# Layer 0's second product on four column groups of 32: a four-layer NHWC kernel on one Trainium2 core

## The chip, the cores and the metric

The kernel runs on one core of a Trainium2 chip. The metric is the device time of one execution in microseconds. Beside it there is one profiled execution, from which all rows and views in this document come. Engines are called as in the profile: PE is the matrix engine, PEld its weight loads, DVE, ACT and POOL the three elementwise engines, SP the engine that issues the DMAs.

## What is computed

The input is `x` of 32 images of 56 x 56 tokens with 96 channels, f32, and it goes through four layers. Only layer 0 is touched, and of it only its last product:

```python
rw = sigmoid(mean(x, (1, 2)) @ Wr + br)                 # 4 weights an image
h = relu(bn(x @ mix(rw, Wpw) + ..))                     # 96 -> 384 channels
h = relu(bn(depthwise 3x3 of h, mixed by rw))           # 384 channels
Wk2 = einsum('be,emf->bmf', rw, Wpwl)                   # 384 x 96, one an image
out = bn(h @ Wk2 + ..) + x                              # 384 -> 96, and the shortcut
```

Layer 1 is a depthwise 5x5 filter with a residual, layer 2 a depthwise 3x3 and a pointwise product, layer 3 a shifted-window attention block with a perceptron.

## The kernel before

Every image passes through four stages, each a generator: `stage_router` (the means, the mixed weights), `stage_conditional` (the rest of layer 0), `stage_depthwise` (layers 1 and 2) and `stage_swin` (layer 3). Four images are under way at a time, one in each stage.

**The order of the work** is not that of the code. Every call is recorded as a `Work` with a target, its due time in units of images; `interleave` and `PLAN` (a start and a length for each stage) give these targets. `Recorder.order` then plays all engines through with a table of costs (`COST`, `tensor_time`, `BESIDE`, and the lags `CROSSING` and `TO_TENSOR` between engines) and lets each engine, whenever it is free, begin the ready work with the earliest target whose buffers are available. What comes out is the order in which each engine's instructions are emitted, and on the chip an engine keeps to it. Three rules of this planner matter here:

- Where PE has nothing that could start, the planner emits products of the identity with itself (`banks<-ident` in the profile), whose results nobody reads. I call them spare products.
- An elementwise instruction of DVE over 500 ns that has all its operands in SBUF is never followed by another such: another DVE instruction comes between, or else a memset of one element (`breath`).
- Calls inside `chip.together()` are one piece of work and stay together. PE pays `CHANGE` in the plan when the size of its tiles changes.

**Layer 0's second product.** `stage_conditional` cuts an image into 2 strips of 28 rows. For each strip it makes three blocks of 128 channels, each with nine taps: ACT does the first, DVE the other eight (`h<-h,mix,h`, 128 x 1568). The three blocks of a strip (`h2`, four buffers) are then multiplied with `wmix2`, 3 x (128 x 96), in four pieces of 7 rows, that is 392 columns: `project(n)` accumulates three products of 128 x 96 into one PSUM bank, and `add(n)` lets DVE add the bias and the shortcut out of that bank into `xT`. The generator `projections` yields after each product and after each add, so their targets are spread over the taps of the following block (of the next strip, or after the last one). In f32 one product is two PE records in the trace. All stages draw on one ring of six PSUM banks (`mm` and `cv` are the same ring); the band filters of layers 1 and 2 take four of them at once, the attention scores three. When all pieces of an image are in `xT`, SP copies it in 48 DMAs to the layout of layer 1.

All recorded instructions have line 578 (`Recorder.give`), so in this document they are told apart by their tiles: `banks<-h,wmix` is the second product, `banks<-xT,wmix` the first, `xT<-banks,bias,xT` the add.

Of the kernel before, what the change touches and what calls it, by code (L numbers as in the profile page):

```python
# [19 lines left out]
C = 96  # L20
# [3 lines left out]
P = 128  # L24
NB = 3
NROW = 8
RT = 7 * W
# [17 lines left out]
NSTRIP = H // STRIP  # L45
# [113 lines left out]
LANDING = 2200  # L159
IMAGE_LANDING = 10000  # L160

PLAN = {"router": (-0.309, 1.019), "conditional": (0.642, 1.103), "depthwise": (1.462, 1.483), "swin": (3.316, 0.933)}
CROSSING = 136

TO_TENSOR = {"vector": 981, "gpsimd": 1497, "scalar": 453, "sync": 1437}
SPARE_AFTER = 318
RUN = 1
CHANGE = 170
SAME = 0.0
BESIDE = {(32, 32): 16, (32, 64): 6, (64, 32): 6, (32, P): 3, (P, 32): 3, (P, P): 1}  # L170


def up(n):
# [3 lines left out]
def tiling(call):  # L177
    return tuple(up(n) for n in call[1][1].shape[:1] + (math.prod(call[1][1].shape[1:]),))


def tensor_time(calls):

    tiles = BESIDE[tiling(calls[0])]
    total = 30 if tiles > 1 else 0
# [107 lines left out]
class Recorder:  # L292
# [79 lines left out]
    def order(self):  # L372
# [50 lines left out]
        def done(w, now):  # L423
# [5 lines left out]
            for v in w.after:  # L429
                v.waits -= 1  # L430
                lag = 0 if v.engine == w.engine else TO_TENSOR[w.engine] if v.engine == "tensor" else CROSSING
                v.ready = max(v.ready, now + lag)
# [42 lines left out]
        while left:  # L475
            for e in self.ENGINES:
# [5 lines left out]
                while queues[e] and not unchanged:  # L482
                    item = heapq.heappop(queues[e])
                    w = self.work[item[1]]
                    if not available(w):
                        held.append(item)
                        continue
                    if e == "tensor" and SAME:
                        if first is None:
                            first = item  # L490
                        if item[0] > first[0] + SAME:
                            held.append(item)
# [89 lines left out]
def kernel(  # L582
# [10 lines left out]
    def ring(name, shape, n):  # L593
        return Ring([const.tile(shape, F32, name=f"{name}{k}") for k in range(n)])
# [21 lines left out]
    x1s = ring("x1", [P, NQ, NBLK, W + 4], 2)  # L616
    x2s = ring("x2", [P, NQ, NBLK, W + 2], 2)
    filtereds = ring("filtered", [C + 1, H, W], 1)
    h1s = ring("h1", [P, STRIP + 2, W + 2], 2)
    if general:  # L620
        ss = ring("scores", [PK, NP, PK], 4)
# [55 lines left out]
    for k in range(NB):  # L677
        pt = mm.tiles[k]
# [16 lines left out]
    pt = mm.tiles[3]  # L695
# [31 lines left out]
    pt = mm.tiles[5]  # L727
# [27 lines left out]
    pt = mm.tiles[4]  # L755
# [87 lines left out]
    chip = Recorder(nc)  # L843
# [66 lines left out]
    def stage_conditional(b):  # L910

        xT, wmix, wmix2, mix, bias1, biasd, bias3 = mixed.pop(b)
        h1s_of = {}
        pieces = STRIP // 7

        def expand(strip, k):

            h1 = h1s_of[strip, k] = chip.new(h1s).part(*range(pieces))
            edge = 0 if strip == 0 else STRIP + 1
            chip.gpsimd.memset(h1[:, edge], 0.0)  # L920
            first = max(0, STRIP * strip - 1)
            last = min(H, STRIP * strip + STRIP + 1)
            at = first - (STRIP * strip - 1)
            for piece in range(pieces):
                n = -(-(last - first) // (pieces - piece))
                pt = chip.new(mm)
                chip.tensor.matmul(
                    pt[:, : n * W],
                    wmix[:, k * P : (k + 1) * P],
                    xT[:, first * W : (first + n) * W].part(*range(first // 7, (first + n - 1) // 7 + 1)),  # L930
                    start=True,
                    stop=True,
                )
                chip.scalar.activation(
                    h1[:, at : at + n, 1 : W + 1].part(piece),
                    pt[:, : n * W].rearrange("p (r w) -> p r w", w=W),
                    AF.Relu,
                    bias=bias1[:, k : k + 1],
                    scale=s1[:, k : k + 1],
                )  # L940
                first += n
                at += n
                yield

        def project(n, h2):

            pt = chip.new(mm)
            with chip.together():
                for q in range(NB):
                    chip.tensor.matmul(  # L950
                        pt[:C, :RT],
                        wmix2[:, q * C : (q + 1) * C],
                        h2[q][:, n % pieces * RT : (n % pieces + 1) * RT].part(n % pieces // 2),
                        start=(q == 0),
                        stop=(q == NB - 1),
                    )
            return pt[:C, :RT]

        def add(n, y):
            rows = xT[:, 7 * n * W : 7 * (n + 1) * W].part(n)  # L960
            chip.vector.scalar_tensor_tensor(rows, y, bias3, rows, ALU.add, ALU.add)

        def projections(strip, h2):
            for n in range(pieces * strip, pieces * (strip + 1)):
                y = project(n, h2)
                yield
                add(n, y)
                yield

        blocks = [(strip, k) for strip in range(NSTRIP) for k in range(NB)]
        for _ in expand(*blocks[0]):
            pass
        yield 2
        def relu(acc, k):
            for half in range(2):
                part = acc[:, half * 2 * RT : (half + 1) * 2 * RT].part(half)
                chip.scalar.activation(part, part, AF.Relu, bias=biasd[:, k : k + 1], scale=s2[:, k : k + 1])

        behind = iter(())
        filtered_before = None
        h2 = {}
        for at, (strip, k) in enumerate(blocks):
            ahead = expand(*blocks[at + 1]) if at + 1 < len(blocks) else iter(())
            h1 = h1s_of[strip, k]
            h2[k] = chip.new(h2s).part(0, 1)
            acc = h2[k].rearrange("p (r w) -> p r w", w=W)
            for t in range(9):
                dy, dx = divmod(t, 3)  # L990
                tap = mix[:, k, t : t + 1]
                view = h1[:, dy : dy + STRIP, dx : dx + W]
                if t == 0:
                    chip.scalar.activation(acc, view, AF.Copy, scale=tap)
                else:
                    chip.vector.scalar_tensor_tensor(acc, view, tap, acc, ALU.mult, ALU.add)
                yield 2
                if t % 2 == 0:
                    next(ahead, None)
                    yield 1  # L1000
                if t == 1 and filtered_before:
                    relu(*filtered_before)
                if t > 1:
                    next(behind, None)
                    yield 1
            filtered_before = h2[k], k
            if k == NB - 1:
                for _ in behind:
                    yield 1
                behind = projections(strip, dict(h2))  # L1010
        yield 4
        relu(*filtered_before)
        yield 1
        for _ in behind:
            yield 1
        added[b] = xT
# [579 lines left out]
    def when(stage, b):  # L1596

        start, length = PLAN[stage]
        return b + start, length
# [5 lines left out]
    for step in range(B + 3):  # L1605
        stages = []
        b = step - 3
        if 0 <= b < B:
            stages.append((stage_swin(b, residuals.pop(b)), 148.5, when("swin", b)))
        b = step - 2  # L1610
        if 0 <= b < B:
            residuals[b] = []
            stages.append((stage_depthwise(b, residuals[b]), 49, when("depthwise", b)))
        b = step - 1
        if 0 <= b < B:
            stages.append((stage_conditional(b), 195, when("conditional", b)))
        if step < B:
            stages.append((stage_router(step), 12, when("router", step)))
        interleave(stages)
# [3 lines left out]
def build(nc, shapes, batch):  # L1623

    a = {k: nc.dram_tensor(f"in_{k}", s, F32, kind="ExternalInput").ap() for k, s in shapes.items()}
    layouts = {
        k: nc.dram_tensor(f"in_{k}", s, F32, kind="ExternalInput").ap()
        for k, s in (
            ("mask", (2, PK, NP, PK)), ("keep_last", (P, NP, WT)), ("keep_column", (P, WT)),
            ("k5", (P, NSLOT, 5, 2 * BIN)), ("k3", (P, NSLOT, 3, 2 * BIN)), ("centre", (P, 2 * BIN)),  # L1630
        )
    }

    out = nc.dram_tensor("out", (batch, NROW // 2, 2 * RT, C), F32, kind="ExternalOutput").ap()
    with tile.TileContext(nc) as tc, tc.tile_pool(name="flags", bufs=1) as flags:
        in_range = flags.tile([1, 1], mybir.dt.int32, name="in_range")
        tile_scores_in_range(tc, a, in_range)
        kernel(tc, a, layouts, out, False)

        with tc.If(nc.values_load(in_range[:1, :1]) < 1):  # L1640
            kernel(tc, a, layouts, out, True)
# [23 lines left out]
```

## Time and profile before

| what | value |
|---|---|
| median of 3 runs | 4646.62 us (4646.44 to 4652.35) |
| the profiled execution, its own time | 4639.04 us |
| its span, first to last instruction | 4637.2 us |
| mean granted PE clock | 0.992 of full |
| PE busy | 4489.9 us, 97% |
| DVE busy | 4061.4 us, 88% |
| ACT busy | 3393.6 us, 73% |
| POOL busy | 2967.1 us, 64% |

A group row reads: line, engine, operation, output<-inputs, rows*columns of the PE tile, output shape<-input shape, count | busy us, mean ns of one | idle time of the engine just before them, and what ended most of it. A PE record's duration is a latency through the array; records overlap, so the pace of PE is read from the distance between the starts. A timeline row reads: start us, length us, engine, and a run of equal records, merged. A window row gives, for a stretch of the span, each engine's busy us and, in brackets, its count of instructions.

### The profile page before, as it was taken

The numbers are of one execution on the slowest core, as the hardware profiler recorded it, in microseconds if no ns is written. First come the engines' busy times: TensorE is split into PE (matmuls) and PEld (weight loads), VectorE is DVE, ScalarE is ACT, GpSimd is POOL, SyncE is SP. The second block draws the span as 40 slices with busy tenths as digits, with TensorE's granted clock in tenths as the row PEclk, the third lists the DMA queues.
The fourth block names the chain that finished last, engine by engine and source line by source line (L and its number), as shares of the span: only waits on it lengthen the run. The fifth ranks groups of instructions, "written<-read, shape, count | busy, mean of one in ns | idle before, by whom it ended". The sixth has DMA issues, their size and how long they took to land. (4 is left out here: it accounts for less than half of the span.)

```text
span 4637.2 us, 166483 instructions
## 1 busy us (share of the span) xinstructions
PE 4489.9 (97%) x71978; PEld 3168.6 (68%) x71978; DVE 4061.4 (88%) x5444; ACT 3393.6 (73%) x6625; POOL 2967.1 (64%) x1855
## 2 busy tenths in 40 slices
PE   5799999999999999999999999999999999999999
PEld 3566767676767676666676766666766676766677
DVE  6999999998999998999998999988999999999733
ACT  2467777777777777777787777777777787777666
POOL 3035767666767766767766767766767666767633
PEclk8999999999999999999999999999999999999999
DMA  2112111122111122211121211121211122211110
GB/s 54 34 39 45 41 43 32 39 48 45 44 41 30 38 47 45 45 40 30 38 47 45 46 40 30 38 45 45 46 41 30 38 45 45 46 41 31 28 36 22
DMA packets 556411, 185.36 MB, mean 40 GB/s; under 512 B 551679, under 2 KB 552340, under 8 KB 552596
## 3 DMA queue, kind: packets, MB, share of 16 engines
q1 hardware_dynamic: 555668, 174.61, 16.9%
q8 instruction: 569, 9.32, 0.9%
q14 instruction: 174, 1.43, 0.1%
HBM read 42.37 MB, written 38.54 MB: 17 GB/s over the span
## 5 line engine op out<-in xcount | busy, mean ns | idle before, releaser
L578 DVE SCALAR_TENSOR_TENSOR h<-h,mix,h 128x1568 f32<-128x1568 f32 x1536 | 2892.2, 1890 | 18.7 <-ACT h L578 13.0
L578 POOL TENSOR_TENSOR var<-var,mhalf 112x4 f32<-112x4 f32 (+1 forms) x512 | 1068.8, 2093 | 195.4 <-DVE var L578 182.8
L578 POOL TENSOR_TENSOR lnd<-res,var 112x384 f32<-112x384 f32 (+1 forms) x512 | 779.1, 1528 | 524.7 <-PE banks L578 503.0
L578 ACT ACTIVATE hid<-banks,c 128x448 f32<-128x448 f32 (+1 forms) x768 | 446.4, 589 | 346.5 <-PE banks L578 340.4
L578 PE MATMUL banks<-xT,wmix 96*128 96x392 f32 (+1 forms) x1536 | 644.2, 519 | 5.7 <-DVE wmix L578 4.5
L578 PE MATMUL banks<-hT,w 96*128 96x448 f32 (+1 forms) x1536 | 641.0, 507 | 3.7
L578 PE MATMUL banks<-x,band 32*32 32x280 f32 x24576 | 611.7, 408 | 14.8 <-issue 7.7
L578 PEld LDWEIGHTS banks<-w,hid 128*112 128x112 f32 x5376 | 563.9, 178 | 75.9 <-issue 46.2
L578 POOL TENSOR_TENSOR tb<-res,L_conv_b 112x384 f32<-112x384 f32 (+1 forms) x256 | 506.3, 1994 | 160.0 <-DMA out<-tb 139.1
L578 PE MATMUL banks<-w,hid 128*112 128x96 f32 x5376 | 576.2, 262 | 5.1 <-ACT hid L578 4.6
L578 PE MATMUL banks<-h,wmix 128*96 128x392 f32 x1536 | 548.4, 497 | 11.6 <-ACT h L578 11.6
L578 ACT ACTIVATE h<-banks,bias,s 128x392 f32<-128x392 f32 (+1 forms) x768 | 518.3, 690 | 39.0 <-PE banks L578 29.6
L578 PEld LDWEIGHTS banks<-x,band 32*32 32x32 f32 x24576 | 385.0, 103 | 226.7 <-issue 50.7
L578 POOL TENSOR_TENSOR exps<-exps,keep_column 49x147 f32<-49x147 f32 x224 | 396.2, 1769 | 204.1 <-ACT exps L578 194.0
L578 ACT ACTIVATE h<-h,biasd,s 128x784 f32<-128x784 f32 x384 | 389.3, 1038 | 114.0 <-DVE breath L578 83.6
L578 PEld LDWEIGHTS banks<-h,wmix 128*96 128x96 f32 x1536 | 246.5, 164 | 248.6 <-issue 207.2
L578 PEld LDWEIGHTS banks<-xT,wmix 96*128 96x128 f32 x1536 | 266.0, 192 | 134.0 <-issue 57.6
L578 DVE TENSOR_REDUCE var<-lnsq 112x4 f32<-112x388 f32 (+1 forms) x512 | 253.7, 496 | 113.3 <-ACT lnsq L578 59.8
L578 ACT ACTIVATE h<-h,mix 128x1568 f32<-128x1568 f32 x192 | 308.6, 1607 | 60.4 <-PE banks L578 46.4
L578 DVE SCALAR_TENSOR_TENSOR tb<-banks,res,tb 112x96 f32<-112x96 f32 x896 | 246.6, 308 | 109.2 <-PE banks L578 103.9
L578 PEld LDWEIGHTS banks<-hT,w 96*128 96x128 f32 x1536 | 252.5, 191 | 128.9 <-issue 69.1
L578 PEld LDWEIGHTS banks<-ident,lnd 112*96 112x96 f32 x1792 | 197.5, 126 | 157.0 <-issue 127.3
(135 smaller groups left out, 6653.0 us busy)
## 6 DMA issues: line engine op xcount, KB each, us to landing
x<-xT SPq DMA_DIRECT2D x1536, 35.0 KB
xT<-in_x SPq DMA_DIRECT2D x32, 1176.0 KB
filtered<-x SPq DMA_DIRECT2D x960, 35.0 KB
out<-tb SPq DMA_DIRECT2D x128, 168.0 KB
out<-tb SPq DMA_DIRECT2D x128, 126.0 KB
filtered<-x SPq DMA_DIRECT2D x576, 7.0 KB
band<-in_k SPq DMA_DIRECT2D x1, 960.0 KB
wpw<-in_L_conv_Wpw SPq DMA_DIRECT2D x1, 576.0 KB
```

Source lines behind the costliest of these rows:

```text
L578: getattr(getattr(self.nc, w.engine), method)(*args, **kw)
```

## The change

`project` becomes `round_of`. Three rounds a strip replace the four pieces. In each round PE's columns are four groups of 32. Groups 0 to 2 (PSUM partitions 0 to 95) compute piece r, 32 output channels each; group 3 (partitions 96 to 127) computes 32 channels of the fourth piece, those of group r. After three rounds the fourth piece is complete, spread over three banks. ACT copies its three parts from partitions 96 to 127 into a new SBUF tile `last` (96 x 392, one buffer), and DVE adds it from there. The three rounds of a strip are recorded one after the other, with one target; the adds of the first three pieces and the copies follow at later targets, the add of the fourth piece, but for the last strip, three steps later still. Beside that, seven constants of the planner are changed: the starts and lengths of three stages, the lags, the number of 128 x 32 tiles that go beside each other (3 to 4), and `SAME`, which at 0.0003 lets PE prefer, among work whose targets lie that close, work of the tile size it has.

```diff
-PLAN = {"router": (-0.309, 1.019), "conditional": (0.642, 1.103), "depthwise": (1.462, 1.483), "swin": (3.316, 0.933)}
-CROSSING = 136
+PLAN = {"router": (-0.215, 1.029), "conditional": (0.618, 1.103), "depthwise": (1.457, 1.478), "swin": (3.316, 0.951)}
+CROSSING = 177
-TO_TENSOR = {"vector": 981, "gpsimd": 1497, "scalar": 453, "sync": 1437}
+TO_TENSOR = {"vector": 1024, "gpsimd": 1444, "scalar": 453, "sync": 590}
-SAME = 0.0
-BESIDE = {(32, 32): 16, (32, 64): 6, (64, 32): 6, (32, P): 3, (P, 32): 3, (P, P): 1}
+SAME = 0.0003
+BESIDE = {(32, 32): 16, (32, 64): 6, (64, 32): 6, (32, P): 3, (P, 32): 4, (P, P): 1}
...
+    lasts = ring("last", [C, RT], 1)
...
-        def project(n, h2):
+        def round_of(r, h2):
             pt = chip.new(mm)
             with chip.together():
-                for q in range(NB):
-                    chip.tensor.matmul(
-                        pt[:C, :RT],
-                        wmix2[:, q * C : (q + 1) * C],
-                        h2[q][:, n % pieces * RT : (n % pieces + 1) * RT].part(n % pieces // 2),
-                        start=(q == 0),
-                        stop=(q == NB - 1),
-                    )
-            return pt[:C, :RT]
+                for k in range(NB):
+                    for at in range(pieces):
+                        n, g = (r, at) if at < pieces - 1 else (pieces - 1, r)
+                        chip.tensor.matmul(
+                            pt[32 * at : 32 * at + 32, :RT],
+                            wmix2[:, k * C + 32 * g : k * C + 32 * g + 32],
+                            h2[k][:, n * RT : (n + 1) * RT].part(n // 2),
+                            start=(k == 0),
+                            stop=(k == NB - 1),
+                        )
+            return pt
...
         def projections(strip, h2):
-            for n in range(pieces * strip, pieces * (strip + 1)):
-                y = project(n, h2)
+            last = chip.new(lasts)
+            pts = []
+            for r in range(pieces - 1):
+                pts.append(round_of(r, h2))
+            yield
+            for r, pt in enumerate(pts):
+                chip.scalar.copy(last[32 * r : 32 * r + 32].part(r), pt[32 * (pieces - 1) :, :RT])
+                add(pieces * strip + r, pt[:C, :RT])
                 yield
-                add(n, y)
+            for _ in range(3 if strip < NSTRIP - 1 else 0):
                 yield
+            add(pieces * strip + pieces - 1, last.part(*range(pieces - 1)))
+            yield
```

## The prediction

> **What bounds the kernel now.** I read the page first, for the shares of the engines over the span; then the busy time by windows, for the stretches with different limits; then PE's waits and its group rows in the steady stretch; last PE's timeline, for the pace of single products. The chain of waits ends after one link and says nothing here.
>
> ```profile
> PE 4489.9 (97%) x71978; PEld 3168.6 (68%) x71978; DVE 4061.4 (88%) x5444; ACT 3393.6 (73%) x6625; POOL 2967.1 (64%) x1855
> ...
> PE   5799999999999999999999999999999999999999
> ...
> DVE  6999999998999998999998999988999999999733
> ```
>
> PE is full from the fourth slice to the end. DVE is nearly full for most of that, but idle at the end.
>
> ```profile
> 0.00:120.00 120.00, 64.63 (x298) 47.02 (x298) 81.29 (x163) 38.19 (x50) 34.86 (x37) 0.89 0.21 53
> 120.00:377.00 257.00, 220.95 (x3075) 150.52 (x3074) 244.53 (x270) 140.85 (x251) 60.29 (x49) 0.93 0.16 34
> 377.00:4360.00 3983.00, 3939.52 (x64040) 2764.15 (x64038) 3624.94 (x4775) 3038.99 (x5937) 2758.05 (x1638) 1.00 0.18 41
> 4360.00:4637.00 277.00, 264.82 (x4571) 206.94 (x4570) 110.68 (x239) 175.56 (x391) 113.87 (x132) 0.98 0.12 28
> ```
>
> Up to 377 us the pipeline fills, and DVE is the fuller engine (244.5 of 257 us from 120 on). From 377 to 4360 us PE is busy 98.9%, DVE 91.0%, ACT 76%. The router's reduce `pooled`, one an image, starts first at 560.3 and last at 4170.0 us with 26 images between: a period of 138.8 us. Is the busy PE a needed PE? For 560 to 4170 us:
>
> ```profile
> PE pair L578 <- DVE oT L578: 15.3, 26, 0.6
> PE banks L578 <- issue: 7.2, 17, 0.9
> ...
> L578 PE MATMUL banks<-ident 128*128 128x128 f32 x520 | 67.2, 276 | 0.0
> ```
>
> PE's longest wait in 26 periods sums to 15.3 us, and the spare products take 67.2 us, 2.6 us a period. With the 1.1% of idle time (1.5 us) some 4 of 138.8 us are not needed. So in the steady stretch PE's work sets the period, and work taken off PE shortens it, as long as DVE follows. Where DVE could not is seen inside one period:
>
> ```profile
> 1985.00:2005.00 20.00, 19.95 (x375) 13.01 (x374) 19.31 (x21) 18.40 (x43) 18.38 (x11) 1.00 0.05 10
> 2005.00:2026.00 21.00, 20.30 (x418) 15.60 (x417) 20.18 (x24) 18.26 (x39) 15.67 (x7) 1.00 0.07 16
> 2026.00:2040.00 14.00, 14.00 (x161) 8.02 (x160) 13.44 (x19) 6.26 (x14) 13.07 (x8) 1.00 0.06 14
> ...
> 2108.00:2124.00 16.00, 16.00 (x83) 10.51 (x82) 13.62 (x33) 9.93 (x16) 6.58 (x6) 1.00 0.18 44
> ```
>
> The first three rows are attention: DVE is busy 52.9 of 55 us, and all spare products of this period are there. The second strip's pieces run in the third row (2026 to 2039 us), the first strip's in the last (2108 to 2123 us), where DVE is at 85%.
>
> **PE's time for the product.** The timeline gives its pace now, and that of products on small tiles:
>
> ```profile
> 2026.44 2.14 PE L578 MATMUL banks<-h,wmix 128*96 128x392 f32 x6
> 2028.51 0.55 PE L578 MATMUL pair<-exps,ones 49*32 49x196 f32 x12
> 2028.86 0.66 PE L578 MATMUL pair<-exps,v 49*32 49x49 f32 x48
> ...
> 2054.09 3.88 PE L578 MATMUL banks<-x,band 32*32 32x280 f32 x160
> 2057.91 0.55 PE L578 MATMUL pair<-exps,ones 49*32 49x196 f32 x12
> ...
> 2119.26 4.12 PE L578 MATMUL banks<-h,wmix 128*96 128x392 f32 x12
> 2123.21 0.55 PE L578 MATMUL banks<-ident,lnd 112*96 112x112 f32 x4
> ```
>
> Two pieces, 12 records, take 2123.21 - 2119.26 = 3.95 us, 0.329 us a record, which is 1191 columns a us. A strip (24 records) takes 7.90 us. The piece at 2026.44, followed by another tile size, takes 2.07 us, 0.10 more: the price of one change of size.
>
> After, a strip has 3 rounds x 3 blocks x 4 groups x 2 = 72 records of the same 392 columns. One at a time they would take 23.7 us, four abreast 5.93 us. The trace has no 128 x 32 tile, so these are the bounds. Two rows lie near. The 12 records at 2028.51 (three column groups, two row groups; 196 columns, 0.165 us each) take 0.35 us to the next start: 12 x 0.165 / 0.35 = 5.7 abreast of 6. The 160 band records (all 16 tiles; 280 columns, 0.235 us each) take 3.82 us: 9.8 abreast of 16. But these start 24 ns apart on average, and 16 abreast would need 15 ns; the new ones need only 82 ns, so the pace of issue that may hold the band back does not bear on them. I take four abreast, by the first row. Two changes of size (0.2 us) and the lag of the groups behind one another at the start of a round (the starts of `exps,ones` lie 7 ns apart: under 0.1 us in three rounds) make 6.2 us. **A strip saves 7.9 - 6.2 = 1.7 us of PE, an image 3.4 us.** The weight loads triple in number; those of 32 columns take 103 to 106 ns, beneath passes of 329 ns, as today's of 164 ns are.
>
> A rule speaks against this. The Trainium skill, "TensorE: Matmul & The Clock Gate", section "Measured speedup vs the span model", gives 2.38 times for three column tiles and 3.07 times for four row tiles, not 3 and 4. By 3.07 the rounds would take, as an estimate from that page, 23.7 / 3.07 = 7.7 us and with the changes of size save nothing. The row above, 5.7 of 6 in a run of small-tile products, speaks for the higher figure, but it has three column groups and not four.
>
> **How much of that the end sees.** Of the 64 strips six have their products before 377 us (they start at 98, 150, 199, 247, 297 and 366 us), where DVE sets the pace: nothing. Of the 58 others, 29 first strips lie where DVE has room: 29 x 1.7 = 49 us. The 29 second strips lie in attention, right after the spare products. There a saving turns partly into more spare products unless DVE keeps up, and DVE has 55.0 - 52.9 = 2.1 us to give. I count half: 25 us. Together 74 us.
>
> Does DVE allow it over the whole period? It is busy 126.5 us of these 139 us (all eight windows from 1985 to 2124 us), and would be at 126.5 / 135.6 = 93%. Yes, but with little left.
>
> **The other parts.** *ACT* gets 6 copies an image. The nearest row, 96 x 392 out of a bank, is 0.49 us: 2.9 us an image, into 24% of idle time. If that cover went, 64 x 1.5 = 94 us would be in play; nothing points to it. *DVE* has eight adds as before (0.617 us); two now read SBUF alone, like `hid<-hid,hid` at 0.636 us: +0.04 us an image. They also count as long SBUF operations and each may draw a `breath` of 59 ns: 0.1 us at most. *Banks*: today four banks are taken one after another, each until its add; after, three at nearly one time, each until its copy and its add. Bounds: nothing, or PE waiting a strip for one tap of DVE (1.89 us) to let a bank go. I take nothing, since ACT and the adds empty them in the same order. *`h2`* is released earlier (one yield instead of seven after the strip's end), which can only help. *SP*: the 48 DMAs of an image wait for the last add; its chain becomes longer by a copy of 0.5 us, while the products before it end sooner. Nothing. *The constants* move everything a little. Upwards they can give no more than the 4 us a period that PE doesn't need (29 periods: 116 us). Downwards: the lag from a DMA to PE falls by 847 ns in the plan, and PE may be put to wait for a landing at three band filters and one pointwise product an image, 4 x 0.85 x 29 = 98 us. PE has 43 changes of tile size a period; what `SAME` spares of them is 0.1 us each. I take nothing for the sum, and keep both ends.
>
> **Sum.** The profiled execution took 4639.0 us by its own time (span 4637.2): 4639 - 74 = 4565 us. The median of the runs is 7.6 us above that execution, so 4646.6 - 74 = **4573 us**, 1.6% less.
>
> **The rivals.**
> 1. *Everything is gained*: the planner puts taps of DVE elsewhere, so the second strips gain in full: 58 x 1.7 = 99 us, and some of the 4 us with it: 4520 to 4555 us. For it: DVE idles 12% from 2040 to 2124 us. Against: the attention windows.
> 2. *DVE becomes the bound*, or the rounds are torn apart (six changes of size a strip, 0.4 us lost): 10 to 49 us are left, 4598 to 4636 us. For it: DVE at 96% in attention.
> 3. *Four column groups don't run abreast* (slower). At the band's share, 9.8 of 16, it would be 2.45 abreast: 23.7 / 2.45 + 0.2 = 9.9 us a strip, 2.0 us more than now, 58 x 2.0 = +116 us: 4763 us. It decides below 23.7 / (7.9 - 0.2) = 3.1 abreast. For it: that band row is the only one with four column groups. Against: its pace of issue.
> 4. *PE waits in its fixed order*, for banks or for landings (slower): 58 x 1.89 - 74 = +36 us, 4682 us. For it: full PE gets no time back. Against: PE's waits now sum to under 40 us in 26 periods.
>
> **How the numbers follow.** About the forecast (4555 to 4598) 0.42; rival 1, 0.19; rival 2, 0.14; within 0.2% (9 us, which is about what a measurement of this kernel can tell from no change) 0.07; rival 3, 0.08; rival 4, 0.10. Faster 0.75, same 0.07, slower 0.18. The range from 4515 (rival 1 and a little of the slack) to 4655 leaves out rivals 3 and 4.
>
> **What would show it.** A group `banks<-h,wmix` with 128\*32 and 4608 records; a strip's 72 records in about 6.1 us from first start to next work (right), or over 7.7 us (rival 3). The period from `pooled` at 135 to 137 us. Spare products up from 2.6 us a period by about 1 to 2 us, in attention: the half that I don't count. DVE at 93% in the steady stretch. Rival 4 would stand as idle time of PE, ended by ACT, DVE or a DMA, where now it is 1.5 us a period. The prediction is wrong if the strip takes 6.2 us and the period doesn't fall.

## The result, and the profile after

The changed kernel takes 4767.39 us (median of four runs, 4752.77 to 4775.44), the kernel before beside it 4646.53 us (four runs, 4641.05 to 4652.35). The ratio is 1.0256, 95% interval 1.0232 to 1.0281: **slower by 121 us**, where I forecast 74 us faster. The profiled execution is the longest of the four, 4775.44 us; its span is 4773.6 us, 136 us longer than before's.

First the page's line of busy times and the row of the granted clock:

```profile
PE 4512.6 (95%) x75444; PEld 3159.3 (66%) x75444; DVE 4107.2 (86%) x5130; ACT 3458.0 (72%) x6817; POOL 2530.4 (53%) x1855
...
PEclk8889999999999999899999999999999999999999
```

No engine took over: PE, DVE and ACT all have a smaller share than before, and PE is busy 23 us longer. Then the steady stretch, the same window as in the prediction:

```profile
377.00:4360.00 3983.00, 3838.39 (x65068) 2666.93 (x65067) 3561.43 (x4317) 2998.73 (x5918) 2253.75 (x1580) 0.98 0.18 40
```

From 377 to 4360 us PE is now busy 3838 instead of 3940 us, so it idles 145 instead of 43 us; DVE falls from 91 to 89%.

**The product itself** did what was forecast. PE's timeline has a whole strip:

```profile
2091.05 6.13 PE L578 MATMUL banks<-h,wmix 128*32 128x392 f32 x72
2097.11 0.55 PE L578 MATMUL pair<-exps,ones 49*32 49x196 f32 x12
```

72 records take 6.06 us from their first start to the next work; 72 x 0.329 us one at a time would be 23.7 us, so 3.9 run abreast. The Trainium skill, "TensorE: Matmul & The Clock Gate", section "Measured speedup vs the span model", states 2.38 times for three column tiles and 3.07 for four row tiles. It has no figure for four column tiles; this row lies above both figures, and it decides here.

**The period** did not follow. `pooled` starts at 602.6 us (before 560.3) and, 26 images later, at 4312.2 us (before 4170.0): 142.7 us an image, not 138.8. Before, the 26 distances lie between 137.7 and 140.1 us; after, between 123.2 and 162.8 us. The regular schedule has become an irregular one. The longer period makes 100 us of the 136, the later start 42, the end gives 6 back.

PE's waits between 602 and 4312 us, against the two rows shown in the prediction (us in total, times, longest):

```profile
PE pair L578 <- DVE oT L578: 40.5, 52, 2.5
PE banks L578 <- ACT slots L578: 39.0, 67, 1.4
PE banks L578 <- issue: 19.6, 23, 2.6
PE banks L578 <- ACT hid L578: 15.2, 26, 1.1
```

The wait for `oT` was 15.3 us and never over 0.6 us; `slots` did not appear. The spare products in this stretch rise from 520 records and 67.2 us to 868 and 143.4 us. But for the `issue` row, in which the profile shows nothing that PE waited for, all of this is time in which the order has nothing useful for PE. The clock follows from such places. PE's timeline:

```profile
1948.62 2.25 PE L578 MATMUL banks<-ident 128*128 128x128 f32 x14
1953.15 0.90 PE L578 MATMUL pair<-exps,ones 49*32 49x196 f32 x12 [2.28 <-DVE oT L578]
```

and two windows around it, the last but two columns being the granted clock:

```profile
1944.00:1953.00 9.00, 6.82 (x154) 5.18 (x146) 9.00 (x12) 4.13 (x8) 0.68 (x1) 1.00 0.18 39
1953.00:1960.00 7.00, 6.85 (x88) 6.50 (x89) 6.50 (x7) 2.81 (x6) 4.35 (x1) 0.50 0.26 59
```

At the end of a wait of 2.28 us the clock falls to 0.50, and stays so for 23.9 us. Between 377 and 4350 us the records of the clock show 133 us at one half, before none.

### The profile page after: what moved, and what is told of

It is laid out like the page before. It is cut to its first block, busy times and chain, and to the rows that moved or that the text cites. A ratio compares the mean times of both kernels' runs of the same rounds, so it can differ in the third digit from the quotient of the medians.

```text
span 4773.6 us, 173133 instructions
## 1 busy us (share of the span) xinstructions
PE 4512.6 (95%) x75444; PEld 3159.3 (66%) x75444; DVE 4107.2 (86%) x5130; ACT 3458.0 (72%) x6817; POOL 2530.4 (53%) x1855
## 5 line engine op out<-in xcount | busy, mean ns | idle before, releaser
L578 POOL TENSOR_TENSOR var<-var,mhalf 112x4 f32<-112x4 f32 (+1 forms) x512 | 946.4, 1855 | 502.1 <-DVE var L578 488.5
L578 POOL TENSOR_TENSOR lnd<-res,var 112x384 f32<-112x384 f32 (+1 forms) x512 | 705.6, 1383 | 206.0 <-PE banks L578 194.0
L578 POOL TENSOR_TENSOR exps<-exps,keep_column 49x147 f32<-49x147 f32 x224 | 280.6, 1253 | 622.2 <-ACT exps L578 590.8
L578 ACT ACTIVATE h<-banks,bias,s 128x392 f32<-128x392 f32 (+1 forms) x768 | 507.1, 693 | 102.2 <-PE banks L578 63.5
L578 POOL TENSOR_TENSOR tb<-res,L_conv_b 112x384 f32<-112x384 f32 (+1 forms) x256 | 409.0, 1605 | 305.1 <-DMA out<-tb 221.4
L578 PEld LDWEIGHTS banks<-xT,wmix 96*128 96x128 f32 x1536 | 280.0, 197 | 197.9 <-issue 79.8
L578 PE MATMUL banks<-h,wmix 128*32 128x392 f32 x4608 | 402.3, 496 | 8.3 <-ACT h L578 8.3
L578 PEld LDWEIGHTS banks<-h,wmix 128*32 128x32 f32 x4608 | 141.9, 110 | 243.3 <-issue 210.5
L578 PE MATMUL banks<-ident 128*128 128x128 f32 x1640 | 259.1, 295 | 36.5 <-ACT h L578 23.5
```

The costliest lines, as they stand in the source:

```text
L578: getattr(getattr(self.nc, w.engine), method)(*args, **kw)
```

## The experiments

Theory A: the new constants give a worse order, the product is innocent. Theory B: the new product (rounds kept together, banks held longer, copies by ACT) costs it. Theory C: the order is so sensitive that neither can be blamed alone. Later theories are named where they came up.

**e1, e2: the two halves of the change.** The change moves twelve numbers of the planner: six in `PLAN`, over all four stages, `CROSSING`, three in `TO_TENSOR`, `SAME`, and the 128 x 32 entry of `BESIDE`. e1 is before with all of them but the last, which no tile of it uses; e2 is after with before's constants, but for that entry. The core of e1's edit, which e2 makes the other way round:

```diff
 e1, against before
-PLAN = {"router": (-0.309, 1.019), "conditional": (0.642, 1.103), ...
-CROSSING = 136
+PLAN = {"router": (-0.215, 1.029), "conditional": (0.618, 1.103), ...
+CROSSING = 177
```

> The product as before (four pieces of 128x96 a strip), with all constants of the change. Theory A (the order that the planner makes from the new constants is worse, the product on column groups is not): slower than before, 4720 to 4850 us, with spare products well over the 1246 records of before. Theory B (the rounds themselves, three banks taken at one place, upset the order, and the constants are harmless): 4640 to 4660 us.

> The change's product and its generator, with the constants of before (128x32 tiles still counted as four beside each other). Theory A (constants at fault): faster than before, about 4570 us, as I forecast. Theory B (the rounds upset the order): slower, about as slow as the change, 4750 to 4800 us. Theory C (any edit takes the planner away from an order that fitted the old constants and the old product together): slower than before here and with the old product under the new constants, both by 50 to 200 us.

e1 took 4752.09 us (ratio 1.0232, 1.0209 to 1.0255), e2 4732.62 us (1.0176, 1.0156 to 1.0196). Each half alone loses most of what both lose: +107 and +87 us, together +121. That is C.

**e11: almost nothing changed.** Before, with the start of one stage moved by 0.002 image (0.28 us):

```diff
-"conditional": (0.642, 1.103)
+"conditional": (0.640, 1.103)
```

> The kernel before with one constant moved: the second stage's start in the planner's due times, 0.642 to 0.640 of an image, 0.28 us. The product and everything else stay. Theory C (the order before sits in a narrow spot of the planner's, and any edit leaves it): 4700 to 4770 us, with some 1500 spare records instead of 1246. Rival (the planner is smooth, and only an edit of this size of work matters): 4640 to 4655 us.

4774.12 us, ratio 1.0269 (1.0252 to 1.0286): **as much as the whole change**, with the same product and the same arithmetic. Its page line, and its first wait of PE, which in before is 46.8 us, 16 times:

```profile
PE 4532.2 (95%) x72236; PEld 3202.8 (67%) x72236; DVE 4073.4 (85%) x5208; ACT 3393.6 (71%) x6625; POOL 2814.5 (59%) x1855
```

```profile
PE banks L578 <- ACT h L578: 84.0, 39, 11.8
```

It looks like the change: PE 95%, DVE 85%, no engine full. But it is regular: the distances of `pooled` lie between 142.2 and 145.1 us, so the irregular period of the change is not needed for such a loss. The time of before is the time of one particular order, and a neighbour of it is 128 us slower.

**e12: other constants for the change.** Six constants of after moved a little:

```diff
-PLAN = {"router": (-0.215, 1.029), "conditional": (0.618, 1.103), "depthwise": (1.457, 1.478), "swin": (3.316, 0.951)}
-CROSSING = 177
+PLAN = {"router": (-0.22, 1.013), "conditional": (0.618, 1.103), "depthwise": (1.457, 1.483), "swin": (3.316, 0.951)}
+CROSSING = 174
-TO_TENSOR = {"vector": 1024, "gpsimd": 1444, "scalar": 453, "sync": 590}
+TO_TENSOR = {"vector": 1077, "gpsimd": 1431, "scalar": 453, "sync": 590}
```

> The changed kernel with six of its constants moved a little, chosen so that the planner's own time falls by 38 us, to 12 us under its own time for the kernel before. If the planner's own time tells what the chip does: 4610 to 4650 us. If its time misses what the chip waits for: 4700 to 4780 us, like the change.

4739.08 us, ratio 1.0198 (1.018 to 1.0215): 28 us better than the change, and still 93 us slower than before. The planner's own time, by which this run was to be 12 us faster than before, does not tell what the chip does. Whether some constants make the change faster than before stays open.

**e6, e7: is PE the limit in the change's order?** e6 leaves the third block out of each round; e7 issues each spare product twice.

```diff
 e6
-                for method, args, kw in w.calls:
+                for method, args, kw in w.fewer or w.calls:
...
+            w.fewer = [
+                (method, args, {**kw, "stop": n >= pieces})
+                for n, (method, args, kw) in enumerate(w.calls[: 2 * pieces])
+            ]
 e7
-                for method, args, kw in w.calls:
+                spare = w.engine == "tensor" and w.calls[0][1][1] is w.calls[0][1][2]
+                for method, args, kw in w.calls * (2 if spare else 1):
```

> The changed kernel's order, with the third of the three blocks left out of every round, so the second product lacks a third of its sum. PE loses 24 of 72 records a strip, 2.0 us, 129 us in all. If PE's work still sets the period of the changed kernel: 60 to 115 us off, 4650 to 4705 us. If waits in its order set it: within 30 us of the change, 4740 to 4790 us, with PE's idle time and the half-clock stretches up by as much as the work went down.

> The changed kernel's order, but each of its 820 spare products is issued twice; they stand where the planner sees PE idle. If the half-clock stretches after such places (249 us long, 124 us of clock lost, against 75 and 37 before) are a good part of the loss: under 140 us of half clock, and 4690 to 4740 us. If the waits alone are the loss and the clock follows from them at no price: 4760 us or more, since 820 x 0.26 = 213 us of products are added, part of them in front of work that is ready.

With products of 129 us less for PE, e6 took 4774.45 us (1.0276, 1.0241 to 1.031). With spare products of about 213 us more (820 x 0.26), e7 took 4765.4 us (1.0248, 1.0231 to 1.0265). Neither differs from the change. The pages' first line, PE's alone, of e6 and of e7:

```profile
PE 4472.9 (94%) x73908; PEld 3163.9 (66%) x73908; DVE 4101.0 (86%) x5130; ACT 3458.9 (73%) x6817; POOL 2558.4 (54%) x1855
```

```profile
PE 4609.8 (97%) x77084; PEld 3285.5 (69%) x77084; DVE 4109.3 (86%) x5130; ACT 3456.3 (73%) x6817; POOL 2528.1 (53%) x1855
```

In neither run do PE's products change alone. In e6 the half clock in the steady stretch grows from 133 to 273 us, which is 70 us of pace; in e7 it falls to 34 us, 50 us of pace. PE's busy time, in which both are counted, fell by 40 us in e6 and rose by 97 us in e7, and the time stayed. So in e7 PE is busy 97% of the span, the same share as in before, and yet PE is not what sets the time. What the half clock costs in this order is not shown: e7 takes most of it away and gains nothing, but the added products may have eaten what the clock gave.

**e4, e8: what an engine's time is worth in before's order.** e4 leaves 3 of a strip's 12 products out; e8 leaves the last 2 of 28 rows out of DVE's taps.

```diff
 e4
+            w, kept = chip.work[-1], {2: 2, 3: 1}.get(n % pieces, NB)
...
+                    for q, (method, args, kw) in enumerate(w.calls[:kept])
 e8
+            some, view = acc[:, : STRIP - 2], h1[:, dy : dy + STRIP - 2, dx : dx + W]
```

> Order, tiles and constants of before; of the 12 products of a strip three are left out (one in the third piece, two in the fourth), so layer 0's second product is incomplete there. It takes 6 x 0.329 = 1.98 us of PE a strip away and changes nothing else: the change's saving without its order, its copies and its tile sizes. Theory P (PE sets the period): 58 x 1.98 = 115 us off, 4530 us, or 86 us off if half of the second strips' counts. Theory Q (DVE and POOL set it): under 25 us off, 4620 to 4650 us.

> Order, product and constants of before; the eight taps of DVE leave out the last 2 of a strip's 28 rows, so layer 0's filter is incomplete there. A tap of 1.84 us becomes about 1.71 us: 48 x 0.13 = 6.2 us an image, 200 us in all, less work for DVE, and PE's work is untouched. If PE alone sets the period in that order: under 20 us off, 4625 to 4645 us. If DVE and PE set it in turns, as e4's half gain says: 60 to 110 us off, 4535 to 4585 us.

e4 took 4584.27 us (0.9865, 0.9848 to 0.9881): 61 us for 64 x 1.98 = 127 us of PE, one half. e8 took 4620.82 us (0.9944, 0.9928 to 0.9961): 27 us for the 172 us by which DVE's busy time fell, 0.16. So even in before's order a microsecond taken off PE is worth only half of one.

**e3, e5, e9: the rounds in before's order.** To take the planner out, the engines' order of before is kept and only the content of the second product replaced: the first of a strip's four places stays empty, the other three hold a round each, and the copies and the last add follow.

```diff
 e3
+            chip.work[-1].instead = lambda: round_of(n % pieces - 1, pt, h2)
...
+            calls = [
+                ("scalar", "copy", (last[32 * r : 32 * r + 32], pt[32 * (pieces - 1) :, :RT]), {}),
+                sum_of(n - 1, y),
+            ]
+            return calls + [sum_of(n, last)] * (r == pieces - 2)
 e5, against e3: the add first, the copy 600 ns of the plan later, the last add 600 ns after that
+                if taken or read or (w.engine == "scalar" and w.start >= start + WAIT):
 e9, against e5: five spare products in the empty place of the second strip
+            return [("tensor", "matmul", args, {"start": True, "stop": True})] * (5 if n == pieces else 0)
```

> The order of every engine's work is that of before, instruction for instruction; only in the place of the second, third and fourth piece of a strip PE runs the three rounds of 72 records, the first piece's place stays empty, and ACT's copies stand before the adds. Theory P (PE's work sets the period in the order of before; the change lost by its order alone): 58 x 1.7 = 99 us off if both strips count, 74 us if half of the second strips' saving counts: 4545 to 4575 us. Theory Q (DVE, with the SBUF access that it shares with POOL, sets the period, and PE is only kept full): 4630 to 4655 us.

> As e3, the order of before with the rounds in the places of the pieces, but each round's add comes first, as in the order of before, its copy only before an ACT instruction that is planned at least 600 ns later, and the add of the fourth piece 600 ns after that again. In e3 DVE waited 200 us for the copies, since add and copy of one round read the same bank and the later one waited for the earlier. Theory W (that wait, and the half-clock stretches that follow from it, cost e3 its gain): DVE waits under 40 us for the copies, clock back above 0.985, 4580 to 4610 us, which is what e4 gave (61 us off) less the changes of tile size. Theory Z (the rounds cost something beyond their copies, in PE or in the banks): 4650 to 4730 us.

> As e5, but in the second strip's emptied place, in attention, PE issues five spare products (1.3 us). In e5 PE waits there for DVE, and after it runs at half clock once in nearly every image (211 us in all, against 75). Theory G (the saving becomes idle time there, and the half clock that follows makes a loss of it): under 110 us of half clock, and 4600 to 4645 us. Theory Z (the rounds cost something else): the added products change little or add to it, 4690 to 4730 us.

e3 took 4726.41 us (1.0165, 1.0148 to 1.0182). Its DVE waits, and DVE's timeline in the first strip:

```profile
DVE xT L579 <- ACT last L579: 199.8, 129, 9.5
```

```profile
2096.36 0.62 DVE L579 SCALAR_TENSOR_TENSOR xT<-banks,bias,xT 96x392 f32<-96x392 f32 x1 [2.40 <-ACT last L579]
...
2100.50 0.62 DVE L579 SCALAR_TENSOR_TENSOR xT<-banks,bias,xT 96x392 f32<-96x392 f32 x1 [1.77 <-ACT last L579]
```

The add and the copy of a round only read one bank, but in this program the one recorded second waits for the first. With the copy first, DVE stands still for ACT. In the change this wait is smaller (25.3 us, 34 times, from 602 to 4312 us) because its planner puts the copies elsewhere. e5 takes the wait away and took 4702.76 us (1.0113, 1.0094 to 1.0132). What remains is PE's wait for `oT` (71.1 us, 64 times, before 24.8 us, 35 times): in attention the empty place leaves PE with nothing to do. After it the clock falls:

```profile
2062.65 0.55 PE L610 MATMUL pair<-exps,ones 49*32 49x196 f32 x12 [1.61 <-DVE oT L610]
```

```profile
2064.00:2070.20 6.20, 6.20 (x70) 2.94 (x72) 4.72 (x8) 1.68 (x4) 5.66 (x4) 0.50 0.00 0
```

The half clock in e5's steady stretch is 116 us. e9 differs from e5 by five spare products in that place alone and took **4646.61 us (1.0000, 0.9989 to 1.0011)**; the half clock falls to 7 us. 109 us at half clock are 55 us of pace, and the time fell by 56 us. That the clock is what these spare products bought is inferred from this agreement. In this order they were worth having.

So with before's order kept and the empty place filled, the rounds neither lose nor gain. Where do the 1.8 us a strip go?

**e10: rounds in the first strips alone.**

```diff
+            if n < pieces:
                 chip.work[-1].instead = lambda: round_of(n % pieces - 1, pt, h2)
```

> As e5, but only the first strip of an image has the rounds; the second strip keeps its four pieces as before. Theory G: no idle place arises in attention, half clock as before, and the first strips' saving counts in part: up to 29 x 1.7 = 49 us off, half of it by e4's measure, 4600 to 4625 us. Theory Z: half of e5's loss, about 4675 us.

4645.95 us (0.9993, 0.9979 to 1.0006). I cut each image of the trace into three phases, by the starts of instructions: attention (first to last `qT,kT` product), the MLP (the perceptron, to DVE's last `tb` sum of the image), and the gap to the next image's first `qT,kT`. Means over 25 images of the profiled executions (those of e10 and e17 were the longest of ten), in us:

| kernel | attention | MLP | gap | sum |
|---|---|---|---|---|
| before | 52.75 | 78.08 | 7.90 | 138.7 |
| after | 59.10 | 84.40 | -0.03 | 143.5 |
| e1 | 58.62 | 80.93 | 3.01 | 142.6 |
| e2 | 55.64 | 84.43 | 1.77 | 141.8 |
| e11 | 59.19 | 75.62 | 8.55 | 143.4 |
| e4 | 51.36 | 78.82 | 6.23 | 136.4 |
| e5 | 54.72 | 76.55 | 9.07 | 140.3 |
| e9 | 53.08 | 76.64 | 9.07 | 138.8 |
| e10 | 52.76 | 76.93 | 9.06 | 138.8 |
| e16 | 53.08 | 76.57 | 8.07 | 137.7 |
| e17 | 53.39 | 77.29 | 8.07 | 138.8 |

The table also says where the change's time goes. Its attention is 6.4 us longer than before's and its MLP 6.3 us, and the gap takes back 7.9 us. The constants alone (e1) lengthen above all attention, by 5.9 us, the product alone (e2) above all the MLP, by 6.4 us; in e11 attention is 6.4 us longer and the MLP shorter. From e5 to e9 attention alone is shorter, by 1.6 us: that is where the spare products pay.

In e10 the first strip does save 1.15 us in the MLP, and 1.16 us are given back in the gap. ACT's timeline of e10 around the gap (the image ends at 2134.8 us):

```profile
2137.35 0.48 ACT L610 COPY last<-banks 32x392 f32<-32x392 f32 x1 [1.24 <-DVE xT L610]
...
2142.42 0.46 ACT L610 ACTIVATE lnsq<-res 112x288 f32<-112x288 f32 x1
2142.89 0.48 ACT L610 COPY last<-banks 32x392 f32<-32x392 f32 x1
2143.40 0.49 ACT L610 COPY kT<-banks 96x392 f32<-96x392 f32 x1
```

From 2137 us on ACT has no gap until after this `kT`. The same place in before:

```profile
2122.81 1.60 ACT L578 ACTIVATE h<-h,mix 128x1568 f32<-128x1568 f32 x1 [1.54 <-PE banks L578]
...
2127.25 0.45 ACT L578 ACTIVATE lnsq<-res 112x288 f32<-112x288 f32 x1
2127.60 0.49 ACT L578 COPY kT<-banks 96x392 f32<-96x392 f32 x1
```

In before, `kT` follows `lnsq` directly; in e10 two copies stand ahead. The first waits 1.24 us for DVE's add, but before's ACT stands idle there too, for PE, so with its own 0.48 us it costs only some 0.2 us. The second stands just ahead of `kT` and costs 0.5 us. PE waits for `kT`:

```profile
PE banks L610 <- ACT kT L610: 20.1, 29, 0.8
```

In before no such row is among its waits. New theory: ACT's copies take the saving back.

**e13, e14, e15: the copies held longer.** e13 is e10, e14 is e9, with copies held 6000 ns of the plan; e15 is e10 with 2500 ns.

```diff
-WAIT = 600
+WAIT = 6000
```

> Before's order with rounds in the first strips alone, as in the run that took 4645.95 us, but each copy of a third waits until ACT has a piece of work that is planned at least 6000 ns (instead of 600 ns) after the sum of its round, or until its bank is taken again. Theory (the first strips' saving of 1.25 us an image is taken back by ACT, because the copies stand ahead of the kT copy and ACT waits 1.24 us for DVE at the second copy): PE's wait for ACT at kT, 0.71 us an image before, goes, and most of the 29 x 1.2 = 35 us is kept: 4612 to 4630 us. Rival (the saving is given back by whatever comes next, the copies only happened to stand there): 4640 to 4655 us.

> Rounds in both strips, the idle place in attention filled with five spare products, as in the run that took 4646.61 us, with each copy of a third held for 6000 ns of the plan as in the other run of this call. Theory (ACT's copies stand in the way): faster by about as much as the other one, 4610 to 4630 us, since the first strips save the same there and the second strips' saving goes into the spare products. Rival: 4640 to 4655 us. If holding the copies lets banks come free later than PE needs them, both are slower, with PE or DVE waiting for ACT at a bank.

> As the run with copies held for 6000 ns of the plan and rounds in the first strips alone (4664.46 us), but 2500 ns. Theory (ACT's copies take the saving back: early ones by delaying the kT copy, late ones by keeping their banks from PE): between the two waits both are smaller, 4625 to 4645 us. Rival (what the first strips save is given back by whatever comes next): 4642 to 4660 us.

e13 took 4664.46 us (1.0036, 1.0021 to 1.0051), outside both expectations; e15 4649.34 us (1.0011, 1.0001 to 1.002), inside the rival's and beyond the theory's. The wait for `kT` is gone, and in its place e13 has

```profile
PE banks L610 <- ACT last L610: 41.8, 63, 3.2
```

(e15: 24.4 us, 36 times). A late copy keeps its bank from PE. e14 took 4762.4 us (1.0246, 1.0224 to 1.0269) with 71.6 us of that wait; in it the second strip's last add goes ahead of the held copies, so it adds an older fourth piece, but with the same instructions. These runs alone would also allow the rival, that ACT only happened to stand there.

**e16, e17: no copies at all.** e16 is e10 with each third of the fourth piece added by DVE out of its bank: three adds in the place of one, nothing for ACT. e17 does so in both strips, with e9's five spare products.

```diff
-                ("scalar", "copy", (last[32 * r : 32 * r + 32], pt[32 * (pieces - 1) :, :RT]), {}),
...
+            rows = xT[third, 7 * m * W : 7 * (m + 1) * W]
+            part = (rows, pt[32 * (pieces - 1) :, :RT], bias3[third], rows, ALU.add, ALU.add)
```

> Before's order with rounds in the first strips alone, and no copies by ACT at all: DVE adds each third of the fourth piece straight out of partitions 96 to 127 of its bank, 32 x 392, right behind the sum of its round (three adds of about 0.6 us in the place of one: some 1.2 us more DVE a strip, 38 us in all; by the run with shorter taps a us of DVE is worth 0.13, 5 us). Theory (ACT's copies take the saving back): PE's waits for ACT at kT and at last are gone, 4612 to 4635 us. Rival (the saving is given back by whatever comes next): 4640 to 4660 us.

> As the run with the thirds on DVE (4622.19 us), but with rounds in the second strips too, and five spare products in their emptied place. If the second strips' saving can be had at all in this order: 4590 to 4612 us. If it goes into the spare products, as it did with copies by ACT, and only DVE's 1.2 us more a strip are added in attention, where DVE is busy 52.9 of 55 us: 4620 to 4650 us; above 4640 the second strips' added DVE work has cost about what the first strips saved.

e16 took **4622.19 us (0.9956, 0.994 to 0.9973), faster than both kernels**, than before by 0.4%. PE's two longest waits in it:

```profile
PE banks L610 <- ACT h L610: 47.6, 17, 11.8
PE pair L610 <- DVE oT L610: 24.7, 34, 2.4
```

Neither `kT` nor `last` is among PE's waits, the gap is back at 8.07 us, and 21 of some 35 us (29 x 1.2) are kept, although DVE does 32 x 2 more adds. So ACT's copies were the taker, by their place in ACT's order or by the bank that they hold; e16 removes both. e17 took 4654.44 us (1.0004, 0.9994 to 1.0014): the second strips not only add nothing, they cost e16's gain. PE's wait for `oT` rises from 24.7 to 41.0 us, MLP and attention are both longer than in e16. In this order, rounds as placed here pay in the first strips alone. That does not make PE's time in attention worthless: e4, which leaves work out of a strip's last two pieces, has an attention 1.4 us shorter than before's.

## Why the prediction was wrong

- *PE's time for the product* (7.9 to 6.2 us a strip): right; measured 6.06. Rival 3 (not abreast) is false. Its 4763 us lies next to the result by chance: its mechanism, and the price it put on a strip, did not happen.
- *"So in the steady stretch PE's work sets the period, and work taken off PE shortens it, as long as DVE follows."* Failed. I read it from PE's 98.9% and few waits. In before's order a microsecond of PE is worth one half (e4), in the change's order nothing (e6, e7). What fits this, though no run shows it alone, is an order with chains through ACT and DVE nearly as long as PE's; and the spare products keep PE busy where it has nothing to do.
- *"The constants move everything a little. [...] I take nothing for the sum, and keep both ends."* **This is the step that failed most.** I treated the order as a thing that stays. Constants alone cost 107 us (e1); the product alone, which also brings a new order, cost 87 us where I forecast 74 us less (e2); and a move of 0.28 us in one due time cost 128 us (e11). My downward end, 98 us, was for DMA landings; from 602 to 4312 us PE's waits in the change name no DMA. The loss came as waits on DVE and ACT and as spare products. So the term that I put at nothing was worth 107 us by itself; the forecast missed by 194 us in all (4573 to 4767), and one lag times its uses did not bound what a new order costs.
- *ACT's copies "into 24% of idle time"; "nothing points to it"*. Failed at the place where it counted: in the gap ACT runs without a break, and the copies give back what a first strip saves (e10, e16). The mean share was the wrong view; the timeline at the place of the copies would have shown it.
- *Banks: "I take nothing"*. Half right: in the change's steady stretch no such wait is among PE's large ones, but a held copy does keep its bank from PE (e13 to e15), and the add and the copy of one bank wait for each other (e3).
- *29 second strips count half*. As rounds in before's order they gave nothing (e9, e17): what they save goes into an empty place and into the spare products there (1.3 us of 1.8).
- Rival 4, "PE waits in its fixed order", named the right kind of loss, for banks or landings, and priced it at 36 us slower; by another chain, and at 121 us, it is what came. Rival 1 stood on the same period set by PE and fell with it. Of rival 2, DVE did not become the bound (89% in the steady stretch, not 93%), and the rounds were torn apart only in part: 38 of the 64 strips ran as one block of 72 records, the others in two or three.
- *What would show it*: the strip takes 6.1 us and the period does not fall, which I had named as the sign of being wrong. The spare products rose by 2.9 us a period (2.6 to 5.5), not by 1 to 2.

What stays open: why the order of before is so much better than its neighbours. The runs show that it is better than the two tried with its own product (e1, e11), and in the change where PE waits and which phases are longer, but not which of the moved pieces does it. That a worse order is the whole of the change's loss is inferred from e1, e2 and e11; an order in which the change is faster than before was not found.

## What to carry to other kernels

When an edit goes through a scheduler, its first effect is a new order: price that by moving one constant by almost nothing and by holding the old order fixed with the new work in it, before the edit's own microseconds are summed. A busy share, 97% or 98.9%, doesn't tell whether an engine sets the pace, least of all where filler work exists; take work off it, or add some, and look. Helper work given to an idle engine is judged at its place in the timeline, not by the engine's mean idle share.

## What the runs showed of the hardware

- Four column groups of 128 x 32 f32 products run 3.9 abreast, and their 4608 weight loads (110 ns each) vanish beneath passes of 329 ns.
- The clock fell to 0.50 at the end of a wait of PE of 2.28 us in the change, with PE busy 6.82 of the 9 us before, and the half clock lasted 3.41 us or a multiple of it (3.4, 6.8, 10.2, 17.1, 23.9 us). In e5 a wait of 1.6 us lies within 4 us before 22 of the 24 falls between 377 and 4350 us. The Trainium skill, "TensorE: Matmul & The Clock Gate", Part 1, gives an idle window of about 3.4 us; the lengths of the stretches agree with it, and the waits that were enough here are shorter than its rule of no idle gap above some 3.4 us.
- From e5 to e9, 109 us less at half clock, which are 55 us of pace, came with 56 us less time. In the change's order 99 us less, with spare products added, came with no change of the time (e7).
